# The first chunk's q and k by halves of the tokens, with constants, affine places and the sines' transfers on GpSimd

## The chip, the cores and the metric

The kernel runs on one core of one Trainium2 chip. The metric is the device time of one execution in microseconds (us), lower is better. A core has a matrix engine (TensorE, PE in the profile), a vector engine (VectorE, DVE), a scalar engine for activation functions (ScalarE, ACT), a general engine (GpSimd, POOL) and a sync engine (SyncE, SP) that only issues transfers. Each engine takes its own instructions in order; semaphores make one wait for another. Transfers (DMAs) are issued by SP, ACT or POOL and carried out by 16 shared DMA engines. Matmul results land in PSUM, all other tiles in SBUF, inputs and outputs in DRAM.

## The reference, cut to what matters

One transformer layer: an attention block in which queries, keys and values are sines and cosines of angles made from the normalised input, then a mixture of experts. The change touches only the start of the attention block and one helper of the layer norms.

```python
def _layernorm(x, axis=-1, eps=1e-05):
    m = jnp.mean(x, axis=axis, keepdims=True)
    v = jnp.var(x, axis=axis, keepdims=True)
    return (x - m) / jnp.sqrt(v + eps)

def attn(x, w_q, b_q, phi_q, w_k, b_k, phi_k, w_v, b_v, w_out, b_out):
    B, S, D = x.shape                       # 8, 1024, 512
    H, dh = w_q.shape                       # 16, 32
    t = jnp.arange(S, dtype=x.dtype).reshape(1, S, 1, 1)
    xh = x.reshape(B, S, H, dh)
    theta_q = xh / (1.0 + jnp.abs(w_q)) + b_q + t * phi_q
    sin_q, cos_q = lookup_sin_cos(theta_q)  # table of 2048 steps, linear in between
    Q = jnp.concatenate([cos_q, sin_q], axis=-1)
    theta_k = xh / (1.0 + jnp.abs(w_k)) + b_k + t * phi_k
    sin_k, cos_k = lookup_sin_cos(theta_k)
    K = jnp.concatenate([cos_k, sin_k], axis=-1)
    theta_v = xh / (1.0 + jnp.abs(w_v)) + b_v
    sin_v, cos_v = lookup_sin_cos(theta_v)
    V = cos_v + sin_v
    scores = jnp.einsum('bqhd,bkhd->bhqk', Q, K) / math.sqrt(2 * dh)
    attn = softmax(causal(scores))
    out = jnp.einsum('bhqk,bkhd->bqhd', attn, V).reshape(B, S, D)
    return cos_sin_sum(out / (1.0 + jnp.abs(w_out)) + b_out)

x = x + attn(_layernorm(x), ...)
x = x + moe(_layernorm(x), ...)             # 8 experts, 2 per token, capacity 160 per batch row
```

## The kernel before, in words

The attention work is cut into 32 chunks: 8 batch rows of 1024 tokens times 4 chunks of 128 channels (4 heads). Chunk `n` is batch row `n // 4`, channels `n % 4`. A loop over `n` (lines 1217 to 1357) computes the scores, exponentials and products of chunk `n` while it prepares chunk `n + 1`. Behind it the experts run as a long chain of matmuls. The order on PE, ACT, DVE and SP is the order in which the program writes its instructions (`manual_schedule`, line 121); the order on POOL is chosen by a planner that fills it with whatever is ready in its own estimate of time. So whatever is written ahead of an instruction on its engine holds it up, and generators (`next`, `rest`, `some`) are used to interleave the written order.

What comes ahead of the loop (lines 160 to 347 and 1193 to 1216) has no attention work to hide behind:

- `load_x(0)` loads the first batch row as two tiles of 4 x 128 tokens. The small parameter vectors are loaded on ACT's queue (`vec_in`, `rows_in`); PE transposes `vec_in` and DVE turns it into `vecs` and `inv_qk` (line 213 on). DVE sets the constants, `ones`, `keys_b`, the zero tiles and the second half of the two `v` tiles (lines 177 to 258 and 353).
- `make_base(c)` makes the part of the angle that doesn't depend on the data, position times `phi` plus bias: an iota on POOL, two affine steps on DVE (line 456), two roundings on ACT (458, 459), and after a `yield` the wrapped difference on DVE (461). It is stored in DRAM (`base_d`); `base0` is also kept in SBUF, `base1` is read back from DRAM by `load_base(1)`.
- `layernorm_first` takes the statistics of the 8 token tiles on DVE (404, 405), with the rest of `base0` after the fifth, then `inverse_root` (337 to 345: a guess and four Newton steps of three DVE instructions each), then normalises four tiles on DVE (417) and four on ACT (413). `inverse_root` also serves `layernorm1` (the later batch rows) and `router`.
- `qk_pre(0)` transposes the chunk on PE (line 200) and adds the base on DVE (493); `angle` shifts the turns out (424); ACT takes absolute value, sines and squares (509, 518, 428, 431); `qk_post` multiplies on DVE (434) and sends rows of the result to the `qk` pair tiles by 8 DMAs on SP (533). The same steps run for every chunk; here they run for all 1024 tokens at once, and the scores (608) need the last of these sends.
- `v_pre`, `v_post` do the same for the values. `mask` makes two small masks.

In the loop's first pass, the first scores are followed at once by `v_pre(1)`, two steps of `layernorm1(1, 1)` (which reads the second half of batch row 1, loaded by `load_x(1)`) and `qk_pre(1)`, which needs `base1`.

The helpers that the steps below speak of most:

Of the kernel before, what the change touches and what calls it, by code (L numbers as in the profile page):

```python
# [11 lines left out]
F32 = mybir.dt.float32  # L12
# [9 lines left out]
P = 128  # L22
# [51 lines left out]
def preln_attn_moe_kernel(  # L74
# [84 lines left out]

    vec_in = own.tile([6 * NCH, P], F32, name="vec_in")  # L160
    for i, v in enumerate((w_q, w_k, b_q, b_k, phi_q, phi_k)):
        nc.scalar.dma_start(
            vec_in[i * NCH : (i + 1) * NCH, :], v.rearrange("(c h) d -> c (h d)", h=HPC)
        )
    load_x(0)
# [5 lines left out]
    for i, v in enumerate((w_v, b_v)):  # L171
        nc.scalar.dma_start(rows_in[:, i, :], v.rearrange("(c h) d -> c (h d)", h=HPC))
    nc.scalar.dma_start(rows_in[:, 2, :], b_out.rearrange("(c f) -> c f", c=NCH))
    ident = const.tile([P, P], F32, name="ident")
    make_identity(nc, ident)
    quarter_c = own.tile([P, 1], F32, name="quarter_c")
    nc.vector.memset(quarter_c, math.pi / 2)
    split_c = own.tile([P, 1], F32, name="split_c")
    nc.vector.memset(split_c, -0.5)
    round_c = own.tile([P, 2], F32, name="round_c")  # L180
    for i in range(2):
        nc.vector.memset(round_c[:, i : i + 1], ROUNDT * (1 - 2 * i))

# [28 lines left out]

    ps = two_banks()[:, 0, : 6 * NCH]
    nc.tensor.transpose(ps, vec_in, ident[: 6 * NCH, : 6 * NCH])
    nc.vector.tensor_copy(vecs, ps)

    nc.vector.tensor_copy(inv_qk, vecs[:, : 2 * NCH])
    magnitude(inv_qk)
    nc.vector.tensor_scalar(inv_qk, inv_qk, UNITS, None, ALU.mult)
    magnitude(rows_in[:, 0, :])  # L220
# [9 lines left out]
    for i, t in enumerate((inv_v, bias_v, bias_o)):  # L230
        nc.sync.dma_start(t, rows_d[i].partition_broadcast(P))

    ones = own.tile([P, P], F32, name="ones")
    nc.vector.memset(ones, 1.0)

# [3 lines left out]
    keys_b = own.tile([P, 2, P], BF16, name="keys_b")  # L239
    nc.vector.memset(keys_b, 0.0)  # L240
    later_b = own.tile([P, 2, P], BF16, name="later_b")
# [5 lines left out]
    wr_sb = own.tile([P, NCH, 32], F32, name="wr_sb")  # L247
    nc.vector.memset(wr_sb, 0.0)
    gather_e = own.tile([P, E], F32, name="gather_e")
# [3 lines left out]
    inv_o = own.tile([P, H // 2], F32, name="inv_o")  # L253
    nc.vector.memset(inv_o, 0.0)
    zero = own.tile([P, P], F32, name="vec_in")
    nc.vector.memset(zero, 0.0)
    empty = own.tile([P, E * CAP // P, 2], I32, name="empty")
    nc.vector.memset(empty, 0)

    later = row2.tile([P, NCH, 2 * P], F32, name="xT", bufs=1)[:, :3, :P]  # L260

    def mask():
        for part in range(2):
            for a in range(2):
                r = slice(a * 64, (a + 1) * 64)
                nc.vector.tensor_copy(later_b[r, part, :], later[r, 1 + part - a, :])
                nc.vector.tensor_copy(keys_b[r, part, part * 64 : part * 64 + 64], ident[r, r])

# [62 lines left out]
    def inverse_root(var, name):  # L331

        n = var.shape[1]
        v = small.tile([P, n], F32, name=f"{name}_v")
        y = small.tile([P, n], F32, name=name)
        t = small.tile([P, n], F32, name=f"{name}_t")
        nc.vector.tensor_scalar(v, var, EPS, None, ALU.add)
        nc.vector.tensor_scalar(
            y.bitcast(I32), v.bitcast(I32), -0.5, ROOT_GUESS, ALU.mult, ALU.add
        )  # L340
        nc.vector.tensor_scalar(v, v, -0.5, None, ALU.mult)
        for _ in range(4):
            nc.vector.tensor_tensor(t, y, y, ALU.mult)
            nc.vector.tensor_tensor(t, t, v, ALU.mult)
            nc.vector.scalar_tensor_tensor(y, t, 1.5, y, ALU.add, ALU.mult)
        return y

    v_tiles = []
    for i in range(2):
        vt = vp.tile([P, NTT, HPC, 2 * DH], F32, name=f"v_{i}", tag=f"v_{i}")  # L350


        nc.vector.memset(vt[:, :, :, DH:], 0.0)
        nc.vector.memset(vt[:, :, :, DH : DH + 1], 1.0 / (SUM_UNIT * UNITS))
        v_tiles.append(vt)
# [40 lines left out]

    def layernorm_first(other):


        mv = small.tile([P, NTT, nc.vector.BN_AGGR_DIM], F32, name="mv")  # L400
        tiles = [xn_tiles[0][h][:, t, :] for h in range(2) for t in range(4)]
        for t, xt in enumerate(tiles):
            st = small.tile([P, nc.vector.BN_STATS_DIM], F32, name="st")
            nc.vector.bn_stats(st, xt)
            nc.vector.bn_aggr(mv[:, t, :], st)
            if t == 4:
                rest(other)
        rstd = inverse_root(mv[:, :, 1], "rstd")
        off = small.tile([P, NTT], F32, name="top")
        nc.vector.scalar_tensor_tensor(off, mv[:, :, 0], -1.0, rstd, ALU.mult, ALU.mult)  # L410
        for t, xt in enumerate(tiles):
            if t % 2:
                nc.scalar.activation(
                    xt, xt, AF.Identity, bias=off[:, t : t + 1], scale=rstd[:, t : t + 1]
                )
            else:
                nc.vector.tensor_scalar(
                    xt, xt, mv[:, t, 0:1], rstd[:, t : t + 1], ALU.subtract, ALU.mult
                )
# [21 lines left out]
    def make_base(c):  # L441


        if not room:
            t = xmp.tile([P, NTT, D], F32, name="x_mid").rearrange("p (i t) d -> p i (t d)", i=2)
            room.extend(t[:, i, :].rearrange("p (i s) -> p i s", i=2) for i in range(2))
        p = qkt.tile([P, 2, S], F32, name="qk_base") if c != 1 else room[0]
        r = room[1]
        nc.gpsimd.iota(
            p, pattern=[[0, 2], [1, S]], base=0, channel_multiplier=0,  # L450
            allow_small_or_imprecise_dtypes=True,
        )
        for i in range(2):
            phi = vecs[:, (4 + i) * NCH + c : (4 + i) * NCH + c + 1]
            bias = vecs[:, (2 + i) * NCH + c : (2 + i) * NCH + c + 1]
            nc.vector.tensor_scalar(p[:, i, :], p[:, i, :], phi, bias, ALU.mult, ALU.add)
        if c < 2:
            nc.scalar.activation(r, p, AF.Identity, bias=round_c[:, :1], scale=UNITS)
            nc.scalar.activation(r, r, AF.Identity, bias=round_c[:, 1:])
            yield  # L460
            nc.vector.scalar_tensor_tensor(p, p, UNITS, r, ALU.mult, ALU.subtract)
        else:
            nc.vector.tensor_scalar(p, p, UNITS, None, ALU.mult)
            wrap(p, r)
        nc.sync.dma_start(base_d[c], p)
        if c != 1:
            bases[c] = p

# [8 lines left out]
    def qk_pre(n):  # L477
# [12 lines left out]
        for i in range(2):  # L490
            for a in range(2):
# [4 lines left out]
                )  # L496
            yield p, r


# [694 lines left out]
    base0, base1 = make_base(0), make_base(1)  # L1194
    next(base0)
    rest_of_loads()
    load_x(1)
    layernorm_first(base0)
    next(base1)
    qk_st = rest(qk_pre(0))  # L1200
    angle(*qk_st)
    rest(base1)
    mask()
    v_st = rest(v_pre(0))
    qk_st = rest(absolutes(qk_st))
    qk_sin(qk_st, squares(qk_st[1]))
    pairs = rest(qk_post(qk_st))
    sine(v_st[1])
    square(v_st[0])
    v_post(0, v_st)  # L1210
    magnitude(inv_o)
    load_base(1)
    last = None
# [199 lines left out]
```

## Time and profile before

| | |
|---|---|
| time, median of 3 runs | 3342.53 us (3335.08 to 3347.68) |
| the profiled execution | 3335.3 us, of which its span 3333.5 us |
| busy in the span | PE 96%, weight loads 65%, DVE 69%, ACT 40%, POOL 13% |
| from the span's start to the first score matmul | 52.33 us |
| granted TensorE clock, mean | 0.992 |

The span runs from the first to the last instruction of the core. An engine's busy time is the time in which it runs an instruction. A row such as `L493 DVE SCALAR_TENSOR_TENSOR qk_f<-ps_s,inv_qk,qk_base` names the line of the kernel, the engine, the operation, and the tiles written and read. In the timeline the first number is the start in us from the span's start, the second the length, and the bracket tells how long the engine had been idle before it and what released it. In the waits, the instruction after the engine's name waited for the one behind the arrow; the numbers are the total in us, how often, and the longest.

### The profile page before, as it was taken

The page shows a single profiled execution, that of the slowest core. Times are in us where ns is not written, and L with a number is a line of the kernel's source. Part 1 is how long each engine was busy: PE and PEld are TensorE (multiplying, and loading weights), DVE is VectorE, ACT ScalarE, POOL GpSimd, SP SyncE. Part 2 cuts the span into 40 slices and gives each one's busy share as a digit, 9 for nine tenths or more (in the row PEclk, how much of TensorE's full clock was granted, in tenths as well). Part 3 has the DMA queues.
Part 4 walks back from the last instruction along what each step waited for, and adds up shares of the span by engine and source line. Part 5 has one row for each costly group of instructions (what it writes and reads, how often), then busy time and mean ns, then how long its engine had stood idle before and what let it go on. Part 6 is the DMA issues. An engine that isn't in the chain of part 4 may idle for free.

```text
span 3333.5 us, 48795 instructions
## 1 busy us (share of the span) xinstructions
PE 3201.8 (96%) x18942; PEld 2171.7 (65%) x18942; DVE 2285.6 (69%) x5064; ACT 1320.8 (40%) x1609; POOL 419.3 (13%) x363
## 2 busy tenths in 40 slices
PE   3999999999999999899999999999999999999998
PEld 1444444444444444588688688688688688688687
DVE  7887878788887675746746846845845845845854
ACT  5787888878787874201101101201201201201201
POOL 1000202020111103421011011011011011011010
PEclk9999999999999999999999999999999999999999
DMA  4445453545545343422312322322322422322321
GB/s 142 115 119 168 112 165 96 163 127 154 159 128 153 77 142 78 132 42 73 111 35 73 111 42 67 117 38 64 117 45 58 119 43 60 118 47 60 115 38 26
DMA packets 233966, 320.78 MB, mean 96 GB/s; under 512 B 21528, under 2 KB 154376, under 8 KB 221320
## 3 DMA queue, kind: packets, MB, share of 16 engines
q1 hardware_dynamic: 211120, 275.47, 27.8%
q0 software_dynamic: 22528, 42.18, 7.1%
q8 instruction: 150, 2.46, 0.3%
q14 instruction: 80, 0.66, 0.1%
q10 hardware_dynamic: 88, 0.02, 0.0%
HBM read 188.67 MB, written 61.82 MB: 75 GB/s over the span
## 4 chain that ended last, share of the span: by engine, by line
PE 57%; DVE 3%; DMA 1%; issue 1%; POOL 0%; ACT 0%; SPq 0%; POOLq 0%; DVEq 0%; ACTq 0%
PE ps_p L1084 29%; PE ps_p L1039 25%; PE ps_t L995 1%; PE av L642 1%; PE ps_s L608 1%; DMA slot_d<-token,slot 0%; DMA out_dram<-y,slots 0%; DVE t L1024 0%; DVE t L1023 0%; ACT hid L1071 0%; DVE hid L1067 0%; DMA xg<-xn_d,source 0%; DVE u L1065 0%; DVE hid L1068 0%; DVE hid L1069 0%
## 5 line engine op out<-in xcount | busy, mean ns | idle before, releaser
L628 ACT ACTIVATE e<-ps_s 128x1024 f32<-128x1024 f32 (+1 forms) x640 | 569.1, 938 | 225.0 <-PE ps_s L608 128.0
L608 PE MATMUL ps_s<-qk 64*128 64x512 f32 (+3 forms) x3072 | 599.4, 508 | 56.3 <-DMA qk<-qk_r 21.4
L1084 PE MATMUL ps_p<-w,hid 128*128 128x256 f32 x2560 | 570.6, 380 | 0.0
L1084 PEld LDWEIGHTS ps_p<-w,hid 128*128 128x128 f32 x2560 | 485.3, 191 | 66.7
L642 PE MATMUL av<-e,v 128*64 128x512 f32 (+3 forms) x3072 | 523.9, 490 | 0.0
L1084 PE MATMUL ps_p<-w_t,hid 128*128 128x256 f32 x1920 | 430.0, 379 | 0.0
L608 PEld LDWEIGHTS ps_s<-qk 64*128 64x128 f32 x3072 | 263.8, 189 | 240.8 <-issue 140.6
L1084 PEld LDWEIGHTS ps_p<-w_t,hid 128*128 128x128 f32 x1920 | 361.9, 190 | 47.7
L642 PEld LDWEIGHTS av<-e,v 128*64 128x64 f32 x3072 | 200.6, 137 | 283.5 <-issue 268.0
L1039 PE MATMUL ps_p<-xe_s,t 128*128 128x256 f32 (+1 forms) x1024 | 299.4, 435 | 5.5 <-DVE t L1024 3.4
L1039 PE MATMUL ps_p<-xe,w 128*128 128x256 f32 (+1 forms) x1024 | 302.4, 439 | 1.2 <-issue 1.1
L1039 PE MATMUL ps_p<-xe,t 128*128 128x256 f32 (+1 forms) x1024 | 296.9, 433 | 0.0
L690 POOL DMA_INDIRECT slot_d<-token,slot x128 | 163.9, 1281 | 1013.1 <-issue 431.6
L1113 ACT COPY p<-ps_p 128x256 f32<-128x256 f32 x40 | 14.8, 369 | 614.0 <-PE ps_p L1084 614.0
L1039 PEld LDWEIGHTS ps_p<-xe_s,t 128*128 128x128 f32 x1024 | 194.2, 191 | 90.5 <-DVE t L1024 7.9
L1039 PEld LDWEIGHTS ps_p<-xe,w 128*128 128x128 f32 x1024 | 194.6, 192 | 85.2 <-DVE hid L1057 5.8
L1039 PEld LDWEIGHTS ps_p<-xe,t 128*128 128x128 f32 x1024 | 194.6, 190 | 81.3 <-issue 1.0
L978 POOL DMA_INDIRECT xg<-xn_d,source x80 | 78.3, 979 | 1104.3 <-PE ps_t L995 1024.4
L1106 POOL DMA_INDIRECT out_dram<-y,slots x80 | 126.5, 1581 | 664.2 <-DVE y L1101 528.7
L1054 ACT ACTIVATE p<-ps_p,b_t 128x256 f32<-128x256 f32 (+1 forms) x128 | 65.5, 512 | 330.7 <-DVE y L1100 169.7
L1058 ACT ACTIVATE hid<-hid 128x256 f32<-128x256 f32 (+1 forms) x128 | 60.1, 470 | 322.3 <-DVE hid L1057 322.3
L1071 ACT ACTIVATE hid<-hid,b_more 128x256 f32<-128x256 f32 (+1 forms) x128 | 71.8, 561 | 271.2 <-DVE hid L1070 271.2
(210 smaller groups left out, 3840.9 us busy)
## 6 DMA issues: line engine op xcount, KB each, us to landing
w<-in_L_ffn_W_dram SPq DMA_DIRECT2D x256, 256.0 KB
qk<-qk_c SPq DMA_DIRECT2D x128, 256.0 KB
qk<-qk_r SPq DMA_DIRECT2D x128, 256.0 KB
w<-in_L_ffn_W_dram SPq DMA_DIRECT2D x64, 512.0 KB
qk_base<-base_d SPq DMA_DIRECT2D x29, 1024.0 KB
xn_d<-xn SPq DMA_DIRECT2D x72, 256.0 KB
x_mid<-in_L_attn_x_dram SPq DMA_DIRECT2D x16, 1024.0 KB
out_dram<-x_mid SPq DMA_DIRECT2D x8, 2048.0 KB
```

Of the source, the lines that this page charges most:

```text
L608: nc.tensor.matmul(ps[:, a, at : at + w], lhsT=pair[r, 1, kb * P : (kb + 1) * P], rhs=pair[r, 0, q0 : q0 + w], start=at == 0, stop=not own ...
L628: nc.scalar.activation(e, ps[:, :, :n], AF.Exp, scale=UNIT * UNIT / math.sqrt(2 * DH))
L642: nc.tensor.matmul(av[a * 64 : (a + 1) * 64, q0 - 512 * h :], lhsT=vt[:, kb, 2 * pr + a, :], rhs=es[i][:, a, at : at + w], start=kb == 0, ...
L690: nc.gpsimd.indirect_dma_start(out=slot_d[b], out_offset=bass.IndirectOffsetOnAxis(ap=idx, axis=0), in_=src, in_offset=None,)
L978: nc.gpsimd.indirect_dma_start(out=xg, out_offset=None, in_=xn2_d[i % 2], in_offset=bass.IndirectOffsetOnAxis(ap=source[:, e, j0 + j, None ...
L995: nc.tensor.transpose(ps[:, c, :], xg[:, c * P : (c + 1) * P], ident)
L1039: nc.tensor.matmul(ps, lhsT=weights[:, k, :], rhs=rows[:, k, :], start=k == 0, stop=k == 1)
L1054: nc.scalar.activation(p1, product(b11, a11), AF.Identity, bias=b1_t[:, e * NHC + q : e * NHC + q + 1])
L1058: nc.scalar.activation(h11, h11, AF.Relu)
L1071: nc.scalar.activation(h12, h12, AF.Relu, bias=more)
L1084: nc.tensor.matmul(ps, lhsT=hs[k][:, part, cols], rhs=ws[k][weight], start=k == 0, stop=k == NHQ - 1,)
L1106: nc.gpsimd.indirect_dma_start(out=out, out_offset=bass.IndirectOffsetOnAxis(ap=meta[:, e, jj[r], 0:1], axis=0), in_=ys[r], in_offset=None ...
```

## The change

Ahead of the loop the order is rewritten, and work is moved from DVE to POOL. The small vectors of the values and of the output are loaded before those of q and k. The constants, zero tiles, the `v` tiles' second halves, the mask copies and, for the first two bases, the affine steps go to POOL. The statistics of the first token tile come first on DVE, those of the other seven as soon as the vectors are done, and the finish of `base0` after the normalisation. Base 1 is kept in SBUF and no longer read back. A new function `qk_first` makes the first chunk's q and k by halves of 512 tokens; of its sends, the cosines' go out on SP's queue and the sines' on POOL's. `load_x(1)` is written behind `qk_first`. `inverse_root` takes three Newton steps where it took four, everywhere.

```diff
-    vec_in = own.tile([6 * NCH, P], F32, name="vec_in")
-    for i, v in enumerate((w_q, w_k, b_q, b_k, phi_q, phi_k)):
-        nc.scalar.dma_start(
-            vec_in[i * NCH : (i + 1) * NCH, :], v.rearrange("(c h) d -> c (h d)", h=HPC)
-        )
     load_x(0)
...
     nc.scalar.dma_start(rows_in[:, 2, :], b_out.rearrange("(c f) -> c f", c=NCH))
+    vec_in = own.tile([6 * NCH, P], F32, name="vec_in")
+    for i, v in enumerate((w_q, w_k, b_q, b_k, phi_q, phi_k)):
+        nc.scalar.dma_start(
+            vec_in[i * NCH : (i + 1) * NCH, :], v.rearrange("(c h) d -> c (h d)", h=HPC)
+        )
...
-    nc.vector.memset(quarter_c, math.pi / 2)
+    nc.gpsimd.memset(quarter_c, math.pi / 2)
...
-    ps = two_banks()[:, 0, : 6 * NCH]
-    nc.tensor.transpose(ps, vec_in, ident[: 6 * NCH, : 6 * NCH])
-    nc.vector.tensor_copy(vecs, ps)
...
+    first_mv = small.tile([P, NTT, nc.vector.BN_AGGR_DIM], F32, name="mv")
+    first_tiles = [xn_tiles[0][h][:, t, :] for h in range(2) for t in range(4)]
+
+    def first_stats(t0, t1):
+        for t in range(t0, t1):
+            st = small.tile([P, nc.vector.BN_STATS_DIM], F32, name="st")
+            nc.vector.bn_stats(st, first_tiles[t])
+            nc.vector.bn_aggr(first_mv[:, t, :], st)
+
+    first_stats(0, 1)
     magnitude(rows_in[:, 0, :])
...
+    ps = two_banks()[:, 0, : 6 * NCH]
+    nc.tensor.transpose(ps, vec_in, ident[: 6 * NCH, : 6 * NCH])
+    nc.vector.tensor_copy(vecs, ps)
...
-    nc.vector.memset(ones, 1.0)
+    nc.gpsimd.memset(ones, 1.0)
...
-                nc.vector.tensor_copy(later_b[r, part, :], later[r, 1 + part - a, :])
-                nc.vector.tensor_copy(keys_b[r, part, part * 64 : part * 64 + 64], ident[r, r])
+                nc.gpsimd.tensor_copy(later_b[r, part, :], later[r, 1 + part - a, :])
+                nc.gpsimd.tensor_copy(keys_b[r, part, part * 64 : part * 64 + 64], ident[r, r])
...
-        for _ in range(4):
+        for _ in range(3):
             nc.vector.tensor_tensor(t, y, y, ALU.mult)
...
-        nc.vector.memset(vt[:, :, :, DH:], 0.0)
-        nc.vector.memset(vt[:, :, :, DH : DH + 1], 1.0 / (SUM_UNIT * UNITS))
+        nc.gpsimd.memset(vt[:, :, :, DH:], 0.0)
+        nc.gpsimd.memset(vt[:, :, :, DH : DH + 1], 1.0 / (SUM_UNIT * UNITS))
...
-    def layernorm_first(other):
+    def layernorm_first():
...
-            if t == 4:
-                rest(other)
...
+        affine = nc.gpsimd.tensor_scalar if c < 2 else nc.vector.tensor_scalar
...
-            nc.vector.tensor_scalar(p[:, i, :], p[:, i, :], phi, bias, ALU.mult, ALU.add)
+            affine(p[:, i, :], p[:, i, :], phi, bias, ALU.mult, ALU.add)
         if c < 2:
-            nc.scalar.activation(r, p, AF.Identity, bias=round_c[:, :1], scale=UNITS)
-            nc.scalar.activation(r, r, AF.Identity, bias=round_c[:, 1:])
-            yield
-            nc.vector.scalar_tensor_tensor(p, p, UNITS, r, ALU.mult, ALU.subtract)
+            rs = [r[:, i, :] for i in range(2)]
+            if c == 1:
+
+                rs = [
+                    ep.tile([P, 2, 512], F32, name="e_512", bufs=8).rearrange("p a n -> p (a n)")
+                    for _ in range(2)
+                ]
+            for i in range(2):
+                nc.scalar.activation(
+                    rs[i], p[:, i, :], AF.Identity, bias=round_c[:, :1], scale=UNITS
+                )
+                nc.scalar.activation(rs[i], rs[i], AF.Identity, bias=round_c[:, 1:])
+                yield
+            for i in range(2):
+                nc.vector.scalar_tensor_tensor(
+                    p[:, i, :], p[:, i, :], UNITS, rs[i], ALU.mult, ALU.subtract
+                )
...
         nc.sync.dma_start(base_d[c], p)
-        if c != 1:
-            bases[c] = p
+        bases[c] = p
...
+    def qk_first():
+
+
+        base = bases.pop(0)
+        f, r = (qkt.tile([P, 2, S], I32, name=name) for name in ("qk_f", "qk_r"))
+        c = qkt.tile([P, 2, S], F32, name="qk_c")
+        pairs = [qkp.tile([P, 2, S], F32, name="qk") for _ in range(2)]
+        halves = [slice(h * 512, (h + 1) * 512) for h in range(2)]
+        for h, hs in enumerate(halves):
+            ps = two_banks()
+            for t in range(4):
+                by_halves(ps[:, :, t * 64 : (t + 1) * 64], xn_tiles[0][h][:, t, :P])
+            for i in range(2):
+                for a in range(2):
+                    cols = lambda t: t[:, i, hs].rearrange("p (t a q) -> p t a q", a=2, q=64)[
+                        :, :, a, :
+                    ]
+                    nc.vector.scalar_tensor_tensor(
+                        cols(f), ps[:, a, :256].rearrange("p (t q) -> p t q", q=64),
+                        inv_qk[:, i * NCH : i * NCH + 1], cols(base), ALU.mult, ALU.add,
+                    )
+            angle(f[:, :, hs], r[:, :, hs])
+        for hs in halves:
+            nc.scalar.activation(c[:, :, hs], r[:, :, hs], AF.Abs)
+            nc.scalar.activation(
+                c[:, :, hs], c[:, :, hs], AF.Sin, bias=quarter_c, scale=-STEP_ACT
+            )
+            for i in range(2):
+                square(f[:, i, hs])
+            sine(r[:, :, hs])
+        v = v_pre(0)
+        next(v)
+        for hs in halves:
+            for i, t in enumerate((c, r.bitcast(F32))):
+                times(t[:, :, hs], f[:, :, hs], t[:, :, hs])
+                send = (nc.sync, nc.gpsimd)[i].dma_start
+                for pr in range(2):
+                    for a in range(2):
+                        src = slice((2 * pr + a) * DH, (2 * pr + a + 1) * DH)
+                        dst = slice(a * 64 + i * DH, a * 64 + (i + 1) * DH)
+                        send(pairs[pr][dst, :, hs], t[src, :, hs])
+            v_st = rest(v) or v_st
+        return pairs, v_st
...
     next(base0)
+    next(base0)
     rest_of_loads()
-    load_x(1)
-    layernorm_first(base0)
+    mask()
+    first_stats(1, NTT)
+    layernorm_first()
+    rest(base0)
     next(base1)
-    qk_st = rest(qk_pre(0))
-    angle(*qk_st)
-    rest(base1)
-    mask()
-    v_st = rest(v_pre(0))
-    qk_st = rest(absolutes(qk_st))
-    qk_sin(qk_st, squares(qk_st[1]))
-    pairs = rest(qk_post(qk_st))
+    pairs, v_st = qk_first()
     sine(v_st[1])
     square(v_st[0])
+    next(base1)
+    load_x(1)
     v_post(0, v_st)
     magnitude(inv_o)
-    load_base(1)
+    rest(base1)
```

More of the change, by code (lines that the diff above doesn't have):

```diff
@@ L176, in preln_attn_moe_kernel @@
     quarter_c = own.tile([P, 1], F32, name="quarter_c")
-    nc.vector.memset(quarter_c, math.pi / 2)
+    nc.gpsimd.memset(quarter_c, math.pi / 2)
     split_c = own.tile([P, 1], F32, name="split_c")
-    nc.vector.memset(split_c, -0.5)
+    nc.gpsimd.memset(split_c, -0.5)
     round_c = own.tile([P, 2], F32, name="round_c")
     for i in range(2):
-        nc.vector.memset(round_c[:, i : i + 1], ROUNDT * (1 - 2 * i))
+        nc.gpsimd.memset(round_c[:, i : i + 1], ROUNDT * (1 - 2 * i))
     warm = own.tile([P, 1], F32, name="warm")
@@ L211, in wrap @@
         nc.vector.tensor_tensor(t, t, spare, ALU.subtract)
-    ps = two_banks()[:, 0, : 6 * NCH]
[L214 to L219, printed above, removed]
+    first_mv = small.tile([P, NTT, nc.vector.BN_AGGR_DIM], F32, name="mv")
[6 more added lines that the diff above has]
+    first_stats(0, 1)
     magnitude(rows_in[:, 0, :])
@@ L231, in preln_attn_moe_kernel @@
         nc.sync.dma_start(t, rows_d[i].partition_broadcast(P))
+    ps = two_banks()[:, 0, : 6 * NCH]
+    nc.tensor.transpose(ps, vec_in, ident[: 6 * NCH, : 6 * NCH])
+    nc.vector.tensor_copy(vecs, ps)
+    nc.vector.tensor_copy(inv_qk, vecs[:, : 2 * NCH])
+    magnitude(inv_qk)
+    nc.vector.tensor_scalar(inv_qk, inv_qk, UNITS, None, ALU.mult)
     ones = own.tile([P, P], F32, name="ones")
-    nc.vector.memset(ones, 1.0)
+    nc.gpsimd.memset(ones, 1.0)
     before = own.tile([P, P], F32, name="before")
     keys_b = own.tile([P, 2, P], BF16, name="keys_b")
-    nc.vector.memset(keys_b, 0.0)
+    nc.gpsimd.memset(keys_b, 0.0)
     later_b = own.tile([P, 2, P], BF16, name="later_b")
@@ L247, in preln_attn_moe_kernel @@
     wr_sb = own.tile([P, NCH, 32], F32, name="wr_sb")
-    nc.vector.memset(wr_sb, 0.0)
+    nc.gpsimd.memset(wr_sb, 0.0)
     gather_e = own.tile([P, E], F32, name="gather_e")
@@ L253, in preln_attn_moe_kernel @@
     inv_o = own.tile([P, H // 2], F32, name="inv_o")
-    nc.vector.memset(inv_o, 0.0)
+    nc.gpsimd.memset(inv_o, 0.0)
     zero = own.tile([P, P], F32, name="vec_in")
-    nc.vector.memset(zero, 0.0)
+    nc.gpsimd.memset(zero, 0.0)
     empty = own.tile([P, E * CAP // P, 2], I32, name="empty")
-    nc.vector.memset(empty, 0)
+    nc.gpsimd.memset(empty, 0)
     later = row2.tile([P, NCH, 2 * P], F32, name="xT", bufs=1)[:, :3, :P]
@@ L395, in layernorm1 @@
                 yield
-    def layernorm_first(other):
[L400 to L405, printed above, removed]
-            if t == 4:
-                rest(other)
+    def layernorm_first():
+        mv = first_mv
         rstd = inverse_root(mv[:, :, 1], "rstd")
@@ L410, in layernorm_first @@
         nc.vector.scalar_tensor_tensor(off, mv[:, :, 0], -1.0, rstd, ALU.mult, ALU.mult)
-        for t, xt in enumerate(tiles):
+        for t, xt in enumerate(first_tiles):
             if t % 2:
```

## The prediction, made before the changed kernel was run

> **What bounds the kernel now.** I read three views: the page's slices, the waits of the first 80 us, and the timelines of the same stretch and of one later pass of the loop.
>
> ```profile
> PE   3999999999999999899999999999999999999998
> DVE  7887878788887675746746846845845845845854
> ```
>
> PE is full in every slice but the first. There, 3 tenths of 83.3 us are work, and this slice is what the change rewrites. The waits say what PE stands for:
>
> ```profile
> PE ps_s L608 <- DMA qk<-qk_r: 21.4, 1, 21.4
> PE ps_s L200 <- DVE xn L417: 20.8, 1, 20.8
> DVE qk_f L493 <- DMA qk_base<-base_d: 7.3, 1, 7.3
> ```
>
> PE does nothing until the tokens are normalised, a few transposes, and nothing again until the sines' rows have landed. The third line is a later stall, in the loop's first pass, where DVE stands for `base1` on its way back from DRAM. The timeline gives the chain in numbers:
>
> ```profile
> 7.26 0.18 DVE L215 COPY vecs<-ps_s 128x24 f32<-128x24 f32 x1 [6.24 <-PE ps_s L214]
> ...
> 15.64 0.68 DVE L404 BATCH_NORM_STATS2 st<-xn 128x6 f32<-128x512 f32 x1
> ...
> 27.39 0.17 DVE L410 SCALAR_TENSOR_TENSOR top<-mv,rstd 128x8 f32<-128x8 f32 x1
> ...
> 44.05 2.28 DVE L434 SCALAR_TENSOR_TENSOR qk_r<-qk_f,qk_r 128x2048 f32<-128x2048 f32 x1
> ...
> 47.52 4.20 SPq L533 DMA_DIRECT2D qk<-qk_r  x4
> ...
> 52.33 2.30 PE L608 MATMUL ps_s<-qk 64*128 64x512 f32 x3 [21.39 <-DMA qk<-qk_r]
> ...
> 61.98 2.94 POOL L449 IOTA qk_base<- 128x2048 f32 x1 [50.04 <-DVE qk_f L493]
> 63.08 2.38 DVE L424 TENSOR_SCALAR t_r<-v_p 128x1024 int32<-128x1024 int32 x1
> 63.26 2.19 ACT L428 ACTIVATE qk_f<-qk_f,split_c 128x1024 f32<-128x1024 uint16 x2 [1.68 <-DVE qk_r L424]
> 69.34 2.08 PE L608 MATMUL ps_s<-qk 64*128 64x384 f32 x8 [5.63 <-ACT e L628]
> ```
>
> To see: DVE is nearly solid from 7.26 to 46.3, then 6.0 us of transfers. And the start at 52.33 is not the point that counts: ACT has done five exponentials by 61.6 and then stands behind the squares of chunk 1 (line 428), which wait for DVE's `angle`, over at 63.17. PE stops with it until 69.34. So I measure the change at 63.17. One thing outside this stretch, in the pass after a batch row's end:
>
> ```profile
> 252.83 1.14 PE L608 MATMUL ps_s<-qk 64*128 64x384 f32 x8 [1.12 <-DVE xT L743]
> 256.28 1.99 PE L608 MATMUL ps_s<-qk 64*128 64x512 f32 x8 [1.63 <-DVE qk_f L493]
> ```
>
> DVE runs there without a gap from 238 to 262, `inverse_root` of the router in it (245.8 to 248.7), and PE waits for it twice.
>
> **The change, part by part: DVE's chain to the normalisation.** `vec_in` now comes after the three row vectors on ACT's queue. Before, the ninth load of that queue was issued at 6.02 and, by its semaphore, landed at about 8.6; so `vecs` comes at about 9.1 instead of 7.26. DVE uses the time before: statistics of tile 0 (landed at about 3.4) and the row work (8.41 to 11.12, 2.7 us) now run from 3.4 to 6.9, then DVE idles. `vecs` and `inv_qk` take 1.25 as before and `gather_e` 0.2: 10.5. Seven statistics at 0.80 (16.45 to 17.25): 16.1. Gone from between are the memsets and `v` halves (11.10 to 14.2), the two affine steps at 0.79, and `base0`'s 2.29. Newton loses three instructions at 0.20: 2.9 becomes 2.3, so `top` starts at 18.4 instead of 27.39. ACT's four tiles take 2.93 behind it, till 21.6; DVE's 1.91, till 20.4.
>
> **To the sends.** `base0`'s wrap is now here, on the path: two halves at 1.22 (the row of 128x1024 at line 434), till 22.9. The half adds, 128x256 out of PSUM, are not in the trace: they lie between half of line 493's 0.74 and all of it; I take 0.42, what DVE's two-input rows of 128x256 take in the experts (line 1023). First half 1.7 plus `angle` 0.69: 25.2; second half 27.5. ACT must first round `base1`'s first half, two at 1.05, 21.6 to 23.7, under DVE's work. Then a half on ACT is abs 1.05, sine 1.05, two squares of 512 at about 0.66, sine 1.04: 29.6 and 34.1. DVE: `v_pre` 1.27, cosines' product 1.22 and sines' 1.22 after 29.6 give 31.2; bias and `angle` of v 1.9 till 33.1; second half 34.3 and 35.5, where the old one ended at 46.33. The first scores need only the first half's rows, in PSUM before ACT is free.
>
> **To the end of `angle` of chunk 1.** ACT behind 34.1: v's sine and square 2.2, `base1`'s second half 2.1, table 1.28: exponentials from 39.7, five by about 44.5. DVE: `v_post` 1.22 (after the square, 36.3), `inv_o` 0.6, `base1`'s wrap 2.4 after ACT's 38.4: 40.8; `v_pre(1)` 1.24: 42.0. The readback of `base1` is gone, and with it the 7.3. But `load_x(1)` has moved on SP's queue past the base store and the eight cosine sends, and `layernorm1(1, 1)` reads its second tile next on DVE, with the adds of chunk 1 behind it. SP's last sends issue from 34.3, four at 0.6 (the row has 0.58 to 1.3): the loads start at 37 and move from 38. Behind the sines' rest (some 0.35 MB; sends ran at about 250 GB/s with the DMA engines full) come 2.1 MB at about 380 (the rate of these loads before, between 28 and 36): 45. DVE stands 3 us, then 0.87, 1.2, 0.87, 2.72 and 1.23: `angle` ends at about 52.2 instead of 63.17. The gain is 11.0, of which this new wait has kept 3.
>
> **Newton in the loop.** 24 calls lose 0.6 each. The 15 of `layernorm1` run where PE does not wait: nothing, and nothing lost if wrong. The 7 routers inside the loop lie in a DVE run as at 246, with 2.75 us of PE's wait behind it: 7 x 0.6 = 4.2. The last router, 0.3. Bounds 0 and 5.
>
> **What is costed at nothing.** Memsets on POOL are of the sizes it already does (0.41 for 128x384), some 4 us in all, while it waits for `vecs`; the zero transfers that need them on SP have until 30. Mask copies are used at 35. Eight sines' sends: POOL's plain DMAs take 0.63 to 1.04 to issue and land 2.3 to 5.5 later; I take 1.0, so pair 0's last rows land at about 39 to 40, and five exponentials still end before 52: cover some 7 us. Halved rows could move more slowly: same cover, but the loads would be later by what they lose (up to 2). IOTA of `base2`, seen at 61.98, may come among the sends on POOL: 1.85 to 2.94, same cover.
>
> **Affine on GpSimd.** The trace has no such row. With one input it lies between IOTA (1.85 for 2048, so 0.93) and POOL's two-input row (0.74 for 128x256, so 2.9 for 1024); one input is nearer to the first, and I take 1.5. DVE's own 0.79 is gone either way. The Trainium skill, "GPSIMD Engine Reference", 4.1 Engine selection, speaks against the move: use VectorE for elementwise work, about twice as fast, with one input roughly at line rate. By its figures a step is an estimated 0.9 to 2.2. Row and rule differ only inside the cover: POOL starts at 9.1, does two, the masks (about 3) and one more before ACT wants `base1` at 21.6, so up to 3.1 each costs nothing.
>
> **The port.** The trace shows `angle` of v at 2.38 beside an IOTA that took 2.94; alone they take 0.69 and 1.85. The skill's "SBUF — State Buffer", Who interferes with whom and the box on DVE blocking DMA, reads this as one port that the second comer waits for, and says that sends from GpSimd starve for it. By the rule, v's `angle` at 31 to 33 can hold the first sends by 0.7, and POOL's `base1` steps can hold the small two-input instructions of `inverse_root` and the normalisation at 16 to 20, one POOL step (1.5) or two. By the row alone, 1.7. I count nothing for the likeliest case and up to 4 in the range.
>
> **Sum.** 11.0 + 4.5 = 15.5 on the profiled execution: 3335.3 becomes 3319.8. That execution is at the low end of the runs shown, 7.2 under their median; I take the gain from the median: 3327.
>
> **The rivals.** Likeliest, 0.61: the above, 12 to 19 us with its small terms, 3323 to 3331. That straddles 3325.8, where faster by over 0.5% begins (about what a measurement of this kernel can tell from no change); I split it 0.30 to 0.31. Second, 0.20: the new wait for `load_x(1)` does not bite (the loads run ahead of the sines, or the rows move faster): 3.5 more, 19 and up, 3320 to 3324. For it speaks that POOL issues slowly and leaves the engines free; against it that 2.1 MB took some 8 us from issue in the trace. Third, 0.11: port and POOL's order take 4 to 8: 3330 to 3336, within 0.5%. Fourth, 0.03: the edits leave DVE earlier but another wait in the first pass gives it all back: about 3342. Fifth, 0.05, the other side: GpSimd's affine steps become the bound. Ahead of `qk_first` on ACT stand the roundings of `base1`, behind three affine steps in POOL's order; over 3.1 us each, every us costs three. At 8.3 each the whole 15.5 is gone, at 13.8 the kernel is 0.5% slower, 3359. The nearest rows (0.93, 2.9) speak against it; only that the trace lacks the operation for it. I give 0.04 to beyond 3359. Together: faster 0.50, within 0.5% 0.46, slower 0.04. The range takes the second and third and the 6 us that the median may move by itself: 3316 to 3338.
>
> **What would show it.** After: `top` near 18.4, `qk_r`'s last product near 35.5, first score matmul at 35 to 40, five exponentials from about 40, DVE idle before a statistics row of `xn` for 3 us with the load as releaser, no wait on `base_d`, the squares of chunk 1 at 52, PE's waits near 250 shorter by 0.6. POOL affine rows over 3 us, a POOL release ahead of ACT's line 458, or first scores after 45 would prove me wrong.

## The result, and the profile after

The changed kernel takes 3328.14 us (median of 14 runs, 3317.08 to 3337.09) against 3344.15 us before (14 runs, 3335.08 to 3347.68): a ratio of 0.9955, interval 0.9948 to 0.9963, or 12.4 to 17.4 us. The profiled execution took 3330.72 us, its span 3329.0. That is only 4.6 us less than the profiled execution before, because that one had been 8.9 under its median and this one is 2.6 over its own. What follows therefore compares places in the trace, not spans.

The slices, to be held against the two of before:

```profile
PE   3999999999999998899999999999999999999998
DVE  7887878788787675746746846845845845845854
PEclk8999999999999999999999999999999999999999
```

PE's first slice is still 3. The waits of the first 80 us after the change, PE's first and then DVE's (what waited, for what, total us, times, longest):

```profile
PE ps_s L200 <- DVE xn L419: 16.4, 1, 16.4
PE ps_s L667 <- DMA qk<-qk_r: 12.4, 1, 12.4
PE ps_s L236 <- DMA vec_in<-in_L_attn_phi_k_dram: 10.1, 1, 10.1
PE ps_s L667 <- DVE qk_f L508: 7.7, 1, 7.7
...
DVE st L394 <- DMA xn<-in_L_attn_x_dram: 6.8, 1, 6.8
```

The wait for the sines' rows fell from 21.4 to 12.4, but two new ones stand in the list: PE's 7.7 for the adds of chunk 1 (line 508 now), and behind it DVE's 6.8 for the second batch row's tokens. The timeline of the same stretch shows the chain, merged here over DVE, POOL, PE, SP and ACT in order of time:

```profile
10.42 0.18 DVE L237 COPY vecs<-ps_s 128x24 f32<-128x24 f32 x1 [3.31 <-PE ps_s L236]
10.45 0.20 POOL L266 MEMSET vec_in<- 128x128 f32 x1 [8.39 <-PE ps_s L236]
10.64 1.95 DVE L239 COPY inv_qk<-vecs 128x8 f32<-128x8 f32 x1
10.64 1.84 POOL L363 MEMSET v<- 128x1024 f32 x2
12.49 1.86 POOL L452 IOTA qk_base<- 128x2048 f32 x1
12.83 1.54 DVE L205 TENSOR_SCALAR inv_qk<-inv_qk 128x8 f32<-128x8 f32 x1
...
20.70 1.86 POOL L452 IOTA x_mid<- 128x2048 f32 x1
20.74 1.85 DVE L348 TENSOR_SCALAR rstd<-rstd_v 128x8 int32<-128x8 int32 x1
22.89 2.38 POOL L459 TENSOR_SCALAR x_mid<-x_mid,vecs 128x1024 f32<-128x1024 f32 x2
23.12 0.98 DVE L355 SCALAR_TENSOR_TENSOR rstd<-rstd_t,rstd 128x8 f32<-128x8 f32 x1
24.38 0.90 DVE L354 TENSOR_TENSOR rstd_t<-rstd_t,rstd_v 128x8 f32<-128x8 f32 x1
26.12 0.17 DVE L412 SCALAR_TENSOR_TENSOR top<-mv,rstd 128x8 f32<-128x8 f32 x1
...
41.65 1.22 DVE L436 SCALAR_TENSOR_TENSOR qk_r<-qk_f,qk_r 128x1024 f32<-128x1024 f32 x1
42.06 2.44 PE L667 MATMUL ps_s<-qk 64*128 64x512 f32 x3 [12.39 <-DMA qk<-qk_r]
44.31 1.48 SPq L155 DMA_DIRECT2D xn<-in_L_attn_x_dram  x2
55.48 0.69 DVE L394 BATCH_NORM_STATS2 st<-xn 128x6 f32<-128x512 f32 x1 [6.83 <-DMA xn<-in_L_attn_x_dram]
62.23 2.19 ACT L430 ACTIVATE qk_f<-qk_f,split_c 128x1024 f32<-128x1024 uint16 x2 [10.09 <-DVE qk_r L426]
```

Read it from the bottom. The squares of chunk 1, the point at which the prediction measures, start at 62.23: before it was 63.26, so of the 11.0 us that were forecast for this stretch 1.0 came. The first score matmul at 42.06 is 10.3 earlier than before, and that gain is lost again in DVE's wait at 55.48. Further up, five DVE instructions of 8 elements a partition take 0.90 to 1.95 us instead of 0.17, and each ends within about 0.1 us of a POOL instruction beside it (12.59 and 12.48, 14.37 and 14.35, 22.59 and 22.56, 24.10 and 24.08, which is 22.89 plus half of the two affine steps' 2.38, 25.28 and 25.27). Over 0.17 each, that is 6.4 us. In the kernel before, POOL made the iotas of `base0` and `base1` from 1.05 and 3.86 on, ahead of DVE's chain, and none of DVE's instructions of 8 elements took more than 0.20 in the first 28 us.

The pass of the loop at 246, where PE's two waits of before were 1.12 and 1.63:

```profile
250.90 1.14 PE L667 MATMUL ps_s<-qk 64*128 64x384 f32 x8 [0.53 <-DVE xT L802]
254.35 1.99 PE L667 MATMUL ps_s<-qk 64*128 64x512 f32 x8 [1.63 <-DVE qk_f L508]
```

### The profile page after: what moved, and what is told of

Same layout as the page of the kernel before. It is cut to its first block, busy times and chain, and to the rows that moved or that the text cites. A ratio compares the mean times of both kernels' runs of the same rounds, so it can differ in the third digit from the quotient of the medians.

```text
span 3329.0 us, 48774 instructions
## 1 busy us (share of the span) xinstructions
PE 3203.4 (96%) x18942; PEld 2172.0 (65%) x18942; DVE 2272.0 (68%) x4975; ACT 1320.9 (40%) x1617; POOL 429.5 (13%) x397
## 4 chain that ended last, share of the span: by engine, by line
PE 59%; DVE 2%; DMA 1%; issue 0%; ACT 0%; POOL 0%; SPq 0%; POOLq 0%; DVEq 0%; ACTq 0%
PE ps_p L1143 28%; PE ps_p L1098 28%; PE av L701 1%; PE ps_t L1054 1%; PE ps_s L667 1%; DMA out_dram<-y,slots 0%; DMA xg<-xn_d,source 0%; DMA xn_d<-xn 0%; DMA w<-in_L_ffn_W_dram 0%; DVE y L1159 0%; PE ps_s L200 0%; DVE w_t L1009 0%; DVE w L1008 0%; DVE t L1083 0%; DVE u L1185 0%
```

## The experiments

The runs fell in three sessions with a time of before of their own: 3336.88 us in the first (`newton3_alone`, `after_again`, `loadx_early`, `zero_own`), 3337.43 in the second (`before_again`, `base1_kept`, `early_sines_sp`, `best`), 3339.81 in the third (the rest). Ratios are to that time. "Squares" is the start of chunk 1's squares on ACT.

**Is the first stretch what the two profiles say?** Both kernels again, without an edit.

> The kernel before once more, unedited, for a second profile. In the profiles the changed kernel starts the squares of chunk 1 only 1.0 us earlier than before (62.2 against 63.26), and Newton gives 4 to 5, yet the medians differ by 10 to 16. Theory: the first stretch of before is the same in every execution, within 1.5 us, squares at 62 to 64; what is missing sits in differences between executions further on. Rival: the read of base 1 (7.3 us of wait in the first profile) takes longer in most executions than in that one, squares at 66 or later.

> The changed kernel once more, unedited, timed side by side with the edits of this group. The two profiles differ by 4.6 us and the medians by 16. Theory: the profile of before was a fast execution (3335.3 against a median of 3344) with a higher granted clock (0.992 against 0.990), so a second profile of the changed kernel and its times will again lie near 3328 with a ratio near 0.9955, and the first stretch will again end (chunk 1's squares) near 62. Rival: the first stretch varies from run to run, above all the landing of the second batch row's load (55.5 us in the first profile), and this profile shows it 4 us or more earlier.

`before_again`: squares at 62.51, the wait for `base_d` 7.3, `top` at 26.57; 3335.91 us. `after_again`: 3326.92 us, ratio 0.997 (0.9957 to 0.9982); squares at 62.22, `top` at 25.18, the wait for the tokens 7.7. The vectors landed at 9.50 there and not at 10.42, the five small instructions were held for the same 6.4 us, and the tokens were there at 55.5 in both. So the small gain of the first stretch (0.3 in this pair, 1.0 in the first) is no accident of one execution.

**Newton alone.**

```diff
-        for _ in range(4):
+        for _ in range(3):
```

> The kernel before with one edit: inverse_root takes three Newton steps in place of four (24 calls, each three DVE instructions shorter). The theory of the prediction: the seven routers inside the loop each give 0.6 us to PE and the last 0.3, so 4.5 us off, ratio 0.9987, and the start of PE's 400th product moves by nothing in the first 240 us. Rival: DVE has slack everywhere, 0 to 1 us. Second rival: the whole gain of the change (16 us by the medians) sits here and not in the first stretch, because in the profile of the changed kernel the first stretch gave only 1 us at chunk 1's squares; then 10 us or more, ratio under 0.997.

Median 3334.55 us, ratio 0.9993 (0.9985 to 1.0002): by the median alone not separable from nothing. The waits of PE between 100 and 1310 us, where the row of before reads 7.9 in 7 and that of the changed kernel 3.9 in 7, show where it works:

```profile
PE ps_s L608 <- DVE xT L743: 3.8, 7, 0.6
```

At each of the seven routers PE's products gain another 0.5 to 0.7 us on the profile of before: the 7 x 0.6 of the prediction. Attention ends 5.7 us earlier (the place is PE's last product with `v`). Of this, 2.1 stands already ahead of the first router, where the expectation had nothing, because the first stretch is shorter too (by 0.5 because the vectors landed earlier, at 6.80):

```profile
61.67 2.19 ACT L428 ACTIVATE qk_f<-qk_f,split_c 128x1024 f32<-128x1024 uint16 x2 [0.34 <-DVE qk_r L424]
```

With this one edit the squares thus start no later than in the changed kernel (62.23 and 62.22): up to there, its rewritten order gave nothing that Newton alone does not give.

**The tokens' load earlier.** In the changed kernel, `load_x(1)` goes to where `rest_of_loads()` has been issued, on SP ahead of the first chunk's sends:

```diff
     rest_of_loads()
+    load_x(1)
...
     next(base1)
-    load_x(1)
     v_post(0, v_st)
```

> The changed kernel with load_x(1) put back to where it was on SP's queue, behind the small loads and ahead of the sends, so that it is in SBUF by about 35 us. Theory: the wait of 6.8 us of DVE for this load in the first pass goes, nothing else waits there until the transposes of chunk 1 (over at 48.5) and base 1 (47.5), so the squares of chunk 1 start 5 to 6.5 us earlier (about 56) and the time falls by as much against the changed kernel: some 3322, ratio to before 0.9935 to 0.994. Rival: the wait turns into one for the exponentials or for the sends, or the load delays the sends on the shared DMA engines: under 2 us. A further rival: PE's clock, which was granted at half from 56 to 73 us behind the idle stretch, is granted full and adds another 2 to 4 us.

Median 3319.17 us, ratio 0.9949 (0.9936 to 0.9963), 7.7 under the changed kernel in the same session. No wait for the tokens is left. On DVE, two of the small instructions that were held, `top`, and the adds and `angle` that release ACT:

```profile
9.62 0.97 DVE L239 COPY inv_qk<-vecs 128x8 f32<-128x8 f32 x1
...
11.78 1.60 DVE L241 TENSOR_SCALAR inv_qk<-inv_qk 128x8 f32<-128x8 f32 x1
...
20.91 0.17 DVE L412 SCALAR_TENSOR_TENSOR top<-mv,rstd 128x8 f32<-128x8 f32 x1
...
47.11 2.70 DVE L508 SCALAR_TENSOR_TENSOR qk_f<-ps_s,inv_qk,x_mid 128x512 int32<-128x512 f32 x4
49.84 1.23 DVE L426 TENSOR_SCALAR qk_r<-qk_f 128x2048 int32<-128x2048 int32 x1
```

The squares start at 51.10, 11.1 earlier, where 5 to 6.5 had been expected. Of this the load is 6.8; another 5.2 stand already at `top` (20.91 against 26.12), and 1.0 goes back, because the four normalisations behind it took 2.95 instead of 1.91 beside POOL's affine steps. Of the 5.2, 1.0 is an earlier landing of the vectors, and most of the rest is that DVE was held 2.7 us instead of 6.4: the copy at 9.62 for one of the two memsets beside it, where above it was held for both. This goes with the kernel and not with one execution: 6.4 in both executions of the changed kernel and in `early_whole`, 2.7 in `loadx_early`, `early_sines_sp` and `early_newton4`, with the same order of instructions on POOL up to the affine steps of `base1`. What decides it is not shown, so whether moving the load brings it about stays open. The profiled execution is the fastest of its five, 7.4 under their median, and ends attention 15.9 earlier than that of the changed kernel, more than the squares and twice the medians. Two executions of one kernel lay 0.9 apart there (the changed kernel) and 3.3 (before).

**The zero tile in a place of its own.** `zero` shares the buffer of `vec_in`, so its memset on POOL waits until PE has read the vectors (10.45 above, idle 8.39), and the memsets of `v`, the iotas and the affine steps stand in POOL's order behind it.

```diff
-    zero = own.tile([P, P], F32, name="vec_in")
+    zero = own.tile([P, P], F32, name="zero")
```

> The changed kernel with one edit: the zero tile gets a place of its own in place of sharing that of vec_in. In the profile its memset stood on POOL until PE had transposed vec_in (10.45 us), and everything behind it in POOL's order (the v memsets, both iotas, the affine steps) came 8 us late and ran beside DVE's small instructions, of which seven took 0.9 to 1.95 us where 0.17 is usual (about 7 us in all). Theory: POOL's work moves ahead by 8 us, the small instructions are short again, and the last sine product is 5 to 7 us earlier; the load of batch row 1 follows the sends, so the squares of chunk 1 and the time gain the same 4 to 7 us: ratio 0.9935 to 0.9945. Rival: the affine steps of base 1 now meet other DVE instructions and hold them as long (0 to 2 us).

Median 3323.51 us, ratio 0.9961 (0.9948 to 0.9975), 3.4 under the changed kernel; squares at 59.28. On POOL and DVE:

```profile
2.00 0.19 POOL L266 MEMSET zero<- 128x128 f32 x1
2.19 1.83 POOL L363 MEMSET v<- 128x1024 f32 x2
4.04 1.84 POOL L452 IOTA qk_base<- 128x2048 f32 x1
...
22.02 0.17 DVE L412 SCALAR_TENSOR_TENSOR top<-mv,rstd 128x8 f32<-128x8 f32 x1
52.53 0.69 DVE L394 BATCH_NORM_STATS2 st<-xn 128x6 f32<-128x512 f32 x1 [8.01 <-DMA xn<-in_L_attn_x_dram]
```

POOL does the long writes while DVE has little to do. `top` comes 4.1 earlier, 0.9 of it because the vectors landed earlier (9.49), and the wait for the tokens takes 1.2 back: the load moves with the sends it is queued behind. That leaves 2.9 at the squares, where 4 to 7 had been expected. Four small instructions are still held, by 3.2 us in all, now beside the affine steps, so the rival was right in part. By the medians alone, with intervals that overlap, the edit is not separable from the changed kernel.

**Base 1 kept, in the kernel before.** The readback is taken out, nothing else.

```diff
-        if c != 1:
-            bases[c] = p
+        bases[c] = p
...
-    load_base(1)
```

> The kernel before with one edit: base 1 stays in SBUF for chunk 1 and is not read back (it is still stored for the later batch rows). Theory: the 7.3 us of wait in the profile are worth about 1.2 us, since the transposes of chunk 1 were over only at 57.98 and DVE went on at 59.18: squares of chunk 1 at about 62, ratio 0.9993 to 1. Rival: the read is worth its 7.3 us, or more in most executions: ratio 0.998 or less.

Median 3339.45 us, ratio 1.0002 (0.9993 to 1.0012). The wait of 7.3 is gone and another of the same length stands in its place, on PE's transposes; the first line is PE's first score, the second DVE's adds:

```profile
52.95 2.30 PE L607 MATMUL ps_s<-qk 64*128 64x512 f32 x3 [22.93 <-DMA qk<-qk_r]
...
59.23 2.73 DVE L492 SCALAR_TENSOR_TENSOR qk_f<-ps_s,inv_qk,x_mid 128x512 int32<-128x512 f32 x4 [6.72 <-PE ps_s L200]
```

The transposes of chunk 1 are written on PE behind the first scores. They end 6.3 us after the first score starts, and the adds need them. In the kernel before that is 52.33 + 6.3 = 58.6, and `base1` landed for 59.18: the readback cost some 0.5. `newton3_alone` shows the same without this edit: there PE's transposes release the adds at 57.59, 6.3 behind the first score at 51.27.

**The sines' sends on SP again,** in the kernel of `loadx_early`:

```diff
-                send = (nc.sync, nc.gpsimd)[i].dma_start
+                send = nc.sync.dma_start
```

> The changed kernel with load_x(1) early (as in loadx_early) and the sines' sends on SP's queue like the cosines', so that GpSimd sends nothing there. Sixteen sends at about 0.65 on one queue end near 45 in place of 41: first scores later by up to 1 us, those of the second half by 3 to 4. Theory: the five exponentials that count still end before the squares (51 us in loadx_early), so squares and time stay as in loadx_early, within 1 us: the queue is off the path. Rival: GpSimd's queue is what made the first pass short; then the squares come 3 us or more later.

Median 3317.14 us, ratio 0.9931 (0.9917 to 0.9945), not separable from `loadx_early`. First score at 38.25 against 37.89, squares at 50.77 against 51.10. The queue of GpSimd is worth nothing here.

**The halves undone,** in the kernel of `loadx_early`:

```diff
-    pairs, v_st = qk_first()
+    qk_st = rest(qk_pre(0))
+    angle(*qk_st)
+    v_st = rest(v_pre(0))
+    qk_st = rest(absolutes(qk_st))
+    qk_sin(qk_st, squares(qk_st[1]))
+    pairs = rest(qk_post(qk_st))
```

> The kernel of loadx_early, with the first chunk's q and k made for all 1024 tokens at once again by the steps of the kernel before, all eight sends on SP's queue. Theory (the start that counts is the squares of chunk 1, and DVE's chain to the end of angle sets it, not the first score): DVE has its adds till 28.8 and angle till 30.2; on ACT absolute value, sine, squares and sine then take some 8.3, so the sines' product ends at about 41.3 against 38.7, v's product and base1's finish follow ACT, and angle of chunk 1 ends at about 53.5. First score at 46 to 47 against 37.89 there, 8 to 9 us later, but squares at about 53.5 against 51.10, only 2.4 later; the median 2 to 3 us over loadx_early (about 3321.5, ratio near 0.9957). Rival: the earlier first score is worth its whole 8 to 9 us, so the ratio rises to 0.9972 or more and the squares start at 57 or later. Second rival: the halves are worth nothing, squares within 1 us of 51.1.

Median 3327.27 us, ratio 0.9965 (0.9954 to 0.9977). At the squares the rival was right; the ratio lies between the two expectations, 0.9957 and 0.9972. On PE and DVE:

```profile
48.25 2.29 PE L667 MATMUL ps_s<-qk 64*128 64x512 f32 x3 [21.30 <-DMA qk<-qk_r]
...
54.05 2.73 DVE L508 SCALAR_TENSOR_TENSOR qk_f<-ps_s,inv_qk,x_mid 128x512 int32<-128x512 f32 x4 [3.99 <-PE ps_s L200]
```

The squares start at 58.1, 7.0 later: 4.0 is DVE's wait for PE's transposes, 2.5 stand already at `top` (23.39; held 6.4 again, which undoing the halves does not explain), the small rest is the longer chain less the normalisations, which took 1.91 here and 2.95 there. So the first score does count, from the point at which its 5.8 us to the transposes' end outlast DVE's own chain. With halves the score is at 38 and has some 3 us to spare; without them it sets the start.

**The affine steps on DVE again,** in the kernel of `loadx_early`:

```diff
-        affine = nc.gpsimd.tensor_scalar if c < 2 else nc.vector.tensor_scalar
+        affine = nc.vector.tensor_scalar
```

> The kernel of loadx_early, with the four affine steps of the first two bases on DVE again. Theory (DVE's chain sets the start, and what POOL's affine steps hold up there is less than their own price): each step takes 0.79 on DVE, four on the chain, so the squares of chunk 1 start 3.2 later than in loadx_early, at about 54.3, less at most 0.5 for small instructions that no affine step holds any more; the small instructions beside memsets and IOTAs are held as before. Median about 3 us over loadx_early, ratio near 0.9958. Rival (the shared port): the affine steps on POOL cost DVE as much as they take off it, squares within 1 us of 51.1 and the ratio unchanged at 0.995.

Median 3321.19 us, ratio 0.9955 (0.9943 to 0.9968); squares at 52.9, 1.8 later, between the two expectations. DVE pays 1.58 and 1.53 for the steps, and its four normalisations take 1.91 again instead of 2.95 beside POOL's steps: 2.1 net. Some of this is hidden because the vectors landed 1.0 earlier in this execution. So GpSimd's affine steps are worth about two thirds of their price on DVE here, nearer to the theory; the medians alone, 2.0 apart with intervals that overlap, show nothing.

**Four Newton steps again,** in the kernel of `loadx_early`:

```diff
-        for _ in range(3):
+        for _ in range(4):
```

> The kernel of loadx_early, with four Newton steps instead of three. Theory: 0.6 us more at each router in the loop where PE waits for DVE's transposed row (7 times) and 0.6 more ahead of the normalisation: squares of chunk 1 at 51.7, the waits of PE for xT between 100 and 1310 us back at about 8 from about 4, PE's products later by 0.6 more after each router, the end of attention some 4.8 later; median 3 to 6 us over loadx_early, ratio near 0.9963. Rival: in the shorter kernel other waits take the place, and PE's end of attention moves by less than 2 us.

Median 3322.2 us, ratio 0.9963 (0.995 to 0.9976). The wait for `xT` is back:

```profile
PE ps_s L667 <- DVE xT L802: 7.9, 7, 1.2
```

Squares at 52.2 (1.1 later). Attention ends 9.8 later instead of 4.8, for a reason that the expectation lacked. In two of the passes behind a router, at 400 and 1018, PE falls back by 2.9 instead of 0.6. Of this, 0.9 and 0.7 are a longer wait for the next chunk's adds (2.50 and 2.32 against 1.63); the rest, some 1.5, lies in a stretch at half clock. The windows of 395 to 415 us, first `loadx_early`, then this kernel (the last three columns are granted clock, DMA share and GB/s):

```profile
395.00:415.00 20.00, 18.58 (x178) 8.97 (x180) 15.89 (x25) 18.12 (x19) 2.95 (x4) 1.00 0.35 109
395.00:415.00 20.00, 16.65 (x168) 8.70 (x170) 13.60 (x23) 14.41 (x16) 3.69 (x4) 0.91 0.32 107
```

A mean of 0.91 over 20 us is about 3.5 us at half the clock, or some 1.7 us of full clock. Such stretches also stand in both profiles of the kernel before, at 410 and 720 us in both and at 1030 in one, and in the changed kernel at 410 and 1030. They follow a router's wait of PE, and which of the passes have one differs from execution to execution of the same kernel. In the thirteen profiles each such stretch between 200 and 1240 us stands behind a wait of PE for the adds of 1.8 to 3.8 us, against 1.63 in an undisturbed pass; but waits of 3.15 (the kernel before, at 1034) and 3.64 (`after_again`, at 411) stand without one. What makes this wait longer in some passes is not shown. The Trainium skill, "TensorE: Matmul & The Clock Gate", What's actually happening, gives the same length: after an idle window of about 3.4 us the clock is halved, and the windows run free of the program, so the same wait may or may not fall into one. Most of the waits found here are shorter than that window.

**Put together:** `loadx_early` with the zero tile of its own, and, since the kernel calls `layernorm1(1, 1)` both in the loop's first pass and in its third, the first of the two calls dropped:

```diff
-        elif c == 0 and b + 1 < B:
+        elif c == 0 and 0 < b and b + 1 < B:
```

> The changed kernel with load_x(1) early, the zero tile in a place of its own, and the first of the two normalisations of batch row 1's second half left out (it is done in pass 0 and again in pass 2; the second is kept). Theory: against loadx_early (squares at 51.1) the two statistics between the add of v and the adds of chunk 1 go (1.75 us) and POOL's work comes earlier (up to 3 us of DVE's small instructions): squares at 46.5 to 49.5, ratio to before 0.9935 to 0.9945 on this chip. Rival: by then the exponentials or the sends bind (five exponentials end at about 48): squares not before 49, and under 2 us against loadx_early.

Median 3317.67 us, ratio 0.9938 (0.9923 to 0.9953): below both kernels, not separable from `loadx_early`. Squares at 51.83, 0.7 later than in `loadx_early`, where 1.6 to 4.6 earlier had been expected. Affine steps still hold four small instructions, by 3.2 us, and one more is held beside POOL's sends and iota from 38.96 to 42.95:

```profile
10.01 0.99 DVE L205 TENSOR_SCALAR inv_qk<-inv_qk 128x8 f32<-128x8 f32 x1
...
40.57 2.41 DVE L205 TENSOR_SCALAR inv_o<-inv_o 128x8 f32<-128x8 f32 x1
```

The second alone takes more than the 1.75 that the dropped statistics give. The rival had the right size and the wrong cause: ACT's exponentials are over at 47.90, and the squares wait another 3.9 us for DVE's `angle`.

## Why the prediction was right, and where its steps were not

The time was right, 3327 forecast and 3328.14 measured. The working was right for one of its two parts only.

- *Newton in the loop, 4.5.* Right for the seven routers: PE's waits for `xT` fell from 7.9 to 3.9 us, 4.0 of the 4.2 forecast, seen with the edit alone and with it undone. The 0.3 of the last router no run shows.
- *The first stretch, 11.0.* Wrong: 1.0, and 0.3 in the second pair. The losses follow from three terms. The vectors landed for 10.42 instead of 9.1: 1.3 (0.4 in `after_again`). *"I count nothing for the likeliest case"* for the shared port: 6.4. *"DVE stands 3 us"* for the tokens: 6.8, so 3.8 more. Together 11.5; some 1.5 came back in other terms. The prediction's own last sum is 0.3 off, since 45 and the five terms behind it make 51.9 and not 52.2, and it puts the wait for the tokens at 3 in one place and 3.5 in another.
- *The port.* The prediction looked for it between GpSimd's affine steps and small two-input instructions, and those are held (0.98 and 0.90, some 1.5 in all). The larger part, 4.8, is copies and `tensor_scalar`s beside memsets and iotas, which only write. The Trainium skill, "SBUF — State Buffer", Who interferes with whom, has both halves: a VectorE instruction with two SBUF inputs contends with a GpSimd one that reads, while copy and `tensor_scalar` can enter a mode that takes the whole pair of ports. The rows above agree: in `loadx_early` the two-input instructions of `inverse_root` ran at 0.17 beside an iota from 19.71 to 21.57. The prediction applied the second half to `angle` and the normalisation and not to the small copies and `tensor_scalar`s, and in its likeliest case it counted nothing for either half. So the third rival's cause came, 6.4 us where it had 4 to 8, without its time of 3330 to 3336.
- *The memsets on POOL, "while it waits for `vecs`".* Their cover was not there: the one for `zero` waits for the buffer of `vec_in`, so all behind it fell just where DVE's small instructions run. In `zero_own` this place was worth some 3 us at the squares.
- *The load of the tokens.* Its mechanism was foreseen, its size not. SP could issue it only at 44.31, after the second half's cosines, and it landed in time for 55.48, 11.2 later; 8 had been counted from 37. In these 11.2 us the DMA engines moved 3.39 MB at a mean of 303 GB/s, of which the load is 2.1 MB; the sum had 0.35 MB ahead of it and 380 GB/s for the load. The rest was sends of the sines and cosines and, at the end, the store of `base1`, issued at 47.48. With an earlier `top` the wait gets longer (8.0 in `zero_own`), so this term swallows what other edits win until the load is moved.
- *"The start at 52.33 is not the point that counts"* and *"with it the 7.3"*. Half wrong: in the kernel before, the first score sets the start of the squares by way of PE's transposes, and the wait for `base1` hid behind that one (`base1_kept`). This put two things under one cause, and it is the halves that free the adds (`early_whole`).
- *Costed at nothing and right:* the queue of the sines' sends. The affine step took 1.19 against the 1.5 assumed. The fifth rival did not come: no affine step of the changed kernel was near the 3.1 that its cover allows.

What remains open is most of the gain in time. The places in the traces account for 1.0 + 4.0 = 5.0 us in the first pair and 0.3 + 4.0 in the second. Attention ends 4.7 and 7.1 earlier, and behind it the two kernels differ by less than 0.5 in either pair, so the profiled executions hold no further gain. The medians say 12.4 to 17.4 in the first comparison and 6 to 14 in the second. `newton3_alone` makes the gap plain: its profile starts the squares and ends attention earlier than both profiles of the changed kernel (at 1307.2 against 1308.2 and 1309.1), yet its median is 7.6 us higher in the same session, and the intervals of the two ratios do not meet. What the rewritten start gives to the time is thus measured, but no trace here shows where it lies. Longer waits for the adds and stretches at half clock (1.7 us of full clock each) move single executions, and the runs without a profile don't tell where theirs lay. The mean granted clock (0.991 over the 14 runs of the changed kernel, 0.992 in the profile before) can't decide it, because the changed kernel also spends 56 to 72 us at half clock while PE mostly waits. That the number came out right is therefore partly luck: the shown steps are a third of the first comparison's gain and less than half of the second's.

## What to carry to other kernels

In this kernel, what counted when work went to GpSimd was less its own time than which small VectorE instructions ran at that moment: let its long memsets and iotas run where VectorE has nothing critical, and look for shared buffers that hold them back. A load needed soon belongs ahead of the sends on its queue; here moving one line was worth more than the rest of the first stretch, 6.8 us at the squares by the wait alone. A long wait in the profile may only cover another that ends at the same time, so take it away alone before counting it as a gain.

## What the runs showed of the hardware that was not expected

A copy or `tensor_scalar` of 8 elements a partition on VectorE took 1.95 us beside two memsets of 0.92 on GpSimd, 1.85 beside an iota, and 2.41 beside GpSimd's sends and an iota. How much is lost repeats with the kernel and not with the order of instructions on GpSimd: 6.4 in all in two kernels, 2.7 in three others, with the same order up to `base1`'s affine steps; what decides it is open. GpSimd is held the other way round as well: its two affine steps on `base1` took 5.08 us in `loadx_early`, beside DVE's normalisations, `base0`'s wrap and the first adds, against 2.38 in the changed kernel. And in the changed kernel the granted clock is at half from 56 to 72 us; up to 68 PE has only 2.2 us of work and otherwise waits.
